# Seven block products for the global projection, and a new layout of SBUF, in a planned one-core transformer kernel

## The chip, the cores and the metric

The kernel runs as one program on one core of a Trainium2 chip. The metric is the device time of one execution in microseconds (us), from the first to the last instruction and the little that lies around them; the median of three runs stands for the kernel. Everything is fp32.

## What is computed

Eight sequences `x[b]` of 512 tokens by 256 channels pass through a feed-forward stack of two layers, then a global attention, then the same stack once more:

```python
x = x + 0.5 * ffn(layernorm(x))        # two layers, called "first" below
x = x + attn(layernorm(x), weight)     # 16 heads of 16 channels, all 512 x 512 scores
x = x + 0.5 * ffn(layernorm(x))        # the same weights again, "second"

# one layer of ffn
qkv = shift_token(x) @ wqkv            # 256 -> 3 x 512, 8 heads of 64
q, k = rotary(l2norm(q) * qs), rotary(l2norm(k) * ksc)
x = x + local_attention(q, k, v) @ wo  # window of 128 and the 128 before it
x = x + (a * gelu(g)) @ w2 + b2        # a, g = split(layernorm(shift_token(x)) @ w1 + b1), 682 wide

# attn: y = layernorm(x), head h
o_h = softmax(y_h @ y_h.T / 4) @ y     # 512 x 256
out = sum over h of o_h @ weight[256 h : 256 h + 256]
```

`shift_token` moves half of the channels by one token. The kernel uses that `o_h @ weight_h` is `softmax @ (y @ weight_h)`: for each of 8 x 16 = 128 heads it projects y (512 x 256) with a 256 x 256 block of `weight` first, and multiplies by the probabilities afterwards.

## The kernel before, in words

**Three flows of work.** `stream(0)` and `stream(1)` (line 950) each take the blocks (0, first), (2, first), (4, first), (0, second), (6, first), (2, second), (4, second), (6, second), plus the stream's number: stream 0 has the even sequences, stream 1 the odd. A block is a layer norm and two layers; a layer is `attention` (line 588) and `glu` (line 833). `global_heads(b)` (line 971) runs for b = 0 to 7, once sequence b has had its first block; a second block waits until its sequence has been through the global part. So in the first and in the last blocks only the two streams are there, and between them the global heads fill the engines.

**One order, written by a planner.** Everything is first recorded as operations, not issued. `Plan.order` (line 272) then simulates the five engines with fixed prices (`cost`, line 235: for instance a signal between engines at 250 ns, a DMA at 170 bytes a ns of shared pipe) and issues the operations in that order. On the chip each engine runs its own list strictly in order and waits on semaphores. Operations recorded under `plan.together()` are one piece. Rank (the place in the recording, plus `plan.shift`) decides between operations that are ready together. All instructions are issued at line 385, so every row of the profile says L385; tiles are told apart by name. Tiles live in rings (`Ring`, line 94): `bufs` slots under one tag, handed out when the last user of a slot is planned to be done.

**DMAs** all go through the queue of SyncE (SP), in the planned order.

**The global projection.** For head h, `front` (line 990) loads the 256 x 256 weight block (`work_wa`), `scores` makes four 128 x 512 score banks and exponentiates them on ScalarE into `work_e`, and `project(half)` (line 1013), called twice, writes 128 x (2 x 256) products y @ weight_h into one PSUM bank that VectorE copies to `work_xw`. `attend` (line 1032) multiplies the probabilities by `work_xw`, 16 matmuls a head, and VectorE adds the result to x in SBUF. An fp32 matmul is two passes of TensorE, each with its own weight load; a transpose is one pass. So one head has 16 passes for the projection with 256 columns each, 32 of 256 columns in `attend`, and 8 of 512 columns on 16 rows, four side by side, for the scores.

**Near and far.** `far` (line 959) picks, for all but the first and last blocks of a stream, a way of transposing that leaves TensorE out: VectorE transposes blocks of 32 x 32 and DMAs through DRAM (`dram_turned`, `dram_quarters`, `dram_later`) put the blocks in place. In the first and the last block (near), `attention` and `glu` transpose on TensorE against `const_ident`. A near `glu` has 16 transposes: 4 that bring the shifted half to token columns, 4 back (`work z` into `sh`), 8 for the normed input.

**What SBUF holds.** x of six sequences (`LIVE = 6`) stays in SBUF from load to output; both layers' `wqkv`, `wo` and rotary tables stay for the whole run; `w1`, `w2` are loaded anew for each of the 16 steps. The probabilities (`work_p0`, `work_p1`) and the q, k tiles (`work_qn0`, `work_qn1`) have two buffers per stream.

**The start.** Loads go out as x0, the q part of wqkv, the rotary table, the scales of q and k, the vectors, the k and v parts, wo, x1, the weights of glu. The scales lie in buffers of the z ring. GpSimd (POOL) multiplies the table by the scales, four instructions per layer (lines 1089 to 1091); only then does the z buffer with the scales come free for the shifted half of the layer's input, whose first column GpSimd sets to zero (`shifted`, line 531).

Of the kernel before, what the change touches and what calls it, by code (L numbers as in the profile page):

```python
# [31 lines left out]
LAG = 6  # L32
SMALL = 4
LIVE = 6
# [142 lines left out]
class Plan:  # L177
# [94 lines left out]
    def order(self):  # L272
# [50 lines left out]
        while len(order) < len(self.ops):  # L323
            best = None
            for e in self.ENGINES:
                when = []
                hold = min((op.rank for op in candidates[e] if len(op.opens) > 4 and op.ready <= free[e]), default=None)
                for op in candidates[e]:
                    if op.opens:
                        at = slots(op)  # L330
                        if at is None:
                            continue
                        if hold is not None and op.rank > hold and op.opens[0].ring.space == PSUM:
                            continue
                        at = max(at, op.ready, free[e])
                    else:
                        at = max(op.ready, free[e])
                    when.append((at, op))
                if when:
                    t = min(at for at, _ in when)  # L340
                    if best is None or t < best[0]:
                        best = t, e, when
            assert best is not None, "the plan is stuck"
            t, e, when = best
            change = self.MODE.get(mode[e], 0.0) if e == "tensor" else self.TABLE if e == "scalar" else 0.0
            switch = lambda op: change if op.mode is not None and op.mode != mode[e] else 0.0
            near = [c for c in when if c[0] <= t + 40]
            if e == "tensor":
                near = gathered(near, when, t)
            at, op = min(near, key=lambda c: (c[1].rank + (self.STICK[e] if switch(c[1]) else 0), c[0]))  # L350
            candidates[e].remove(op)
            op.start = at + switch(op)
            mode[e] = op.mode or mode[e]
            free[e] = op.start + op.busy
            op.end = op.start + op.done
            if op.calls[0][0] == "dma_start":
                a = op.calls[0][2]["out"]
                pipe = max(pipe, op.start + 2000.0) + elements(a) * a.shape[0] * 4 / 170
                op.end = pipe + 300
            for x in op.opens:  # L360
                _, x.slot = x.ring.free.pop(0)
                x.ring.open(x.stream, x.turn)
            for x in op.tiles:
                x.left -= 1
                x.end = max(x.end, op.end)
                if not x.left:
                    x.ring.free.append((x.end + self.SIGNAL, x.slot))
                    x.ring.free.sort()
            for o in op.before:
                if o.engine != e:  # L370
                    o.ready = max(o.ready, op.end + self.SIGNAL)
                elif e != "tensor":
                    o.ready = max(o.ready, op.end)
            for o in op.before + op.admits:
                o.waits -= 1
                if not o.waits:
                    candidates[o.engine].append(o)
            order.append(op)
# [13 lines left out]
def macaron(ctx: ExitStack, tc: tile.TileContext, x, weight, wqkv, wo, w1, w2, b2, vecs, qk_scales, rotary, out):  # L392
# [10 lines left out]
    xs = {}  # L403

    def load_x(b):
        xs[b] = xpool.tile([P, NT, D], F32, tag="x", name=f"x{b}", bufs=LIVE)
        nc.sync.dma_start(out=xs[b], in_=x[b].rearrange("(t p) c -> p t c", p=P))

    def load_attention(l):

        wq = wpool.tile([P, 2, 3 * INNER], F32, tag=f"wqkv{l}", name=f"wqkv{l}")
        for part in range(3):
            if part == 1:
                load_tables(l)
            cols = slice(part * INNER, (part + 1) * INNER)
            nc.sync.dma_start(out=wq[:, :, cols], in_=wqkv[l, :, cols].rearrange("(k p) f -> p k f", p=P))
        o = wpool.tile([P, NPAIR, D], F32, tag=f"wo{l}", name=f"wo{l}")
        nc.sync.dma_start(out=o, in_=wo[l].rearrange("(k p) f -> p k f", p=P))
        return wq, o
# [21 lines left out]
    tabs = [const.tile([P, NT, 2, 2, DH], F32, tag=f"tab{l}", name=f"tab{l}") for l in range(DEPTH)]  # L441
    scales, vec = [], []

    def load_tables(l):

        if l == 0:
            nc.sync.dma_start(out=tabs[-1].rearrange("p t a s d -> p (t a s d)"), in_=rotary)
        sc = zpool.tile([P, 2, 2, DH], F32, tag=f"z{l}", bufs=2, width=N + 1)
        nc.sync.dma_start(out=sc.rearrange("p a s d -> p (a s d)"), in_=qk_scales[l : l + 1, :].partition_broadcast(P))
        scales.append(sc)  # L450
        ve = const.tile([P, NVEC], F32, tag=f"vec{l}", name=f"vec{l}")
        nc.sync.dma_start(out=ve, in_=vecs[l])
        vec.append(ve)

    load_x(0)
    attention_weights = [load_attention(0)]
    load_x(1)
    glu_weights = [load_glu(0)]
    attention_weights.append(load_attention(1))

# [127 lines left out]
    def attention(k, y, l, far):  # L588
        wqkv_sb, wo_sb = attention_weights[l]
# [4 lines left out]
        v, latest = {}, []  # L594
# [3 lines left out]
        def front(t):  # L598
# [4 lines left out]
            tb = tabs[l][:, t]  # L603
            pair = {}
            for part in (1, 0, 2):
                ps = bank([P, INNER])
                with plan.together():
                    for c, z in ((0, z0), (1, z1)):
                        nc.tensor.matmul(
                            ps, lhsT=z[:, tok], rhs=wqkv_sb[:, c, part * INNER : (part + 1) * INNER], start=(c == 0), stop=(c == 1)  # L610
# [8 lines left out]
                qk = work.tile([P, HEADS, 2, half], F32, tag=f"qn{k}", bufs=2)  # L619
# [32 lines left out]
        def scores(t, pair, rn):  # L652
# [21 lines left out]
            for g in range(2):  # L674
# [25 lines left out]
                if far and t > 0:  # L700
                    plan.ops[-1].after.update(latest)
                heads = slice(4 * g, 4 * g + 4)

                if far:
                    nb = 6 if quarters else 4
                    pg = work.tile([P, 2 * N], F32, tag=f"p{k}", bufs=2, width=2 * N)
# [3 lines left out]
                else:  # L710
                    pg = work.tile([P, 4, nk * P], F32, tag=f"p{k}", bufs=2, width=2 * N)
# [44 lines left out]
        def values(t, probs):  # L756
# [25 lines left out]
            if far:  # L782
                for g in range(2):
                    with plan.together():
# [5 lines left out]
                    latest[g:] = [plan.ops[-1]]  # L790
# [42 lines left out]
    def glu(k, y, step, xb, far):  # L833
# [3 lines left out]
        if far:  # L837
            sh = work.tile([P, NT, P], F32, tag=f"qn{k}", bufs=2)
# [12 lines left out]
        if far:  # L851
            hn = work.tile([P, 2, 4, NT, P // 4], F32, tag=f"p{k}", bufs=2, width=2 * N)
            part = lambda c, t: hn[:, c, :, t, :]
            split = lambda u: u.rearrange("p (b c) -> p b c", c=P // 4)
        else:
            hn = work.tile([P, 2, NT, P], F32, tag=f"p{k}", bufs=2, width=2 * N)
# [22 lines left out]
        for m in range(FULL):  # L879
            if m < 4:  # L880
                if m % 2 == 0:
                    pair = work.tile([P, 2, N], F32, tag=f"p{k}", bufs=2)
                u = pair[:, m % 2]
            else:
                u = work.tile([P, N], F32, tag=f"qn{k}", bufs=2)
# [14 lines left out]
        u = work.tile([P, N], F32, tag=f"qn{k}", bufs=2)  # L900
# [49 lines left out]
    def stream(k, blocks):  # L950

        for n, (b, second) in enumerate(blocks):
            while second and (b, True) not in done:
                next(others, None)
            y = layernorm(xs[b], k)
            yield
            for l in range(DEPTH):
                step = DEPTH * n + l
                far = FAR and 0 < n < len(blocks) - 1
                yield from attention(k, y, l, far)  # L960
                yield from glu(k, y, step, xs[b], far)
# [3 lines left out]
                if l == 0 and n + 1 < len(blocks) and blocks[n + 1][0] not in xs:  # L965
                    load_x(blocks[n + 1][0])
            done.add((b, False))
            if second:
                nc.sync.dma_start(out=out[b].rearrange("(t p) c -> p t c", p=P), in_=xs[b])

    def global_heads(b):
        mv, rstd = layernorm_stats([[xs[b][:, t, :]] for t in range(NT)], gsmall)
        ys = []
        for t in range(NT):
            y = work.tile([P, D], F32, tag="e", bufs=2 * NT, width=N)
            normalize(y, xs[b][:, t, :], mv, rstd, t)
# [10 lines left out]

        def front(h):  # L990

            w = work.tile([P, 2, D], F32, tag="wa", bufs=2)
            nc.sync.dma_start(out=w, in_=weight[h * D : (h + 1) * D, :].rearrange("(c p) f -> p c f", p=P))

# [18 lines left out]
            def project(half):  # L1013
                pv = bank([P, 2, D])
                with plan.together():
                    for i in range(2):
                        s = 2 * half + i
                        for c in range(2):
                            nc.tensor.matmul(
                                pv[:, i, :],  # L1020
                                lhsT=zT[c][:, s * P : (s + 1) * P],
                                rhs=w[:, c, :],
                                start=(c == 0),
                                stop=(c == 1),
                            )
                xv = work.tile([P, 2, D], F32, tag="xw", bufs=4)
                nc.vector.tensor_copy(xv, pv)
                xw.append(xv)

            return es, xw, rsum, (scores, lambda: project(0), lambda: project(1))  # L1030

        def attend(head, t):
# [7 lines left out]
            xt = xs[b][:, t, :]  # L1040
# [5 lines left out]
        for h in range(AH + 1):  # L1046
            for t in range(NT):
                if head is not None:
                    attend(head, t)
                if after is not None and t < 3:  # L1050
# [8 lines left out]
            after = front(h + 1) if h + 1 < AH else None  # L1059

# [28 lines left out]
    for l in range(DEPTH):  # L1089
        for t in range(NT):  # L1090
            nc.gpsimd.tensor_mul(tabs[l][:, t], tabs[-1][:, t], scales[l])
# [77 lines left out]
```

## Time and profile before

| what | value |
|---|---|
| median of 3 runs (lowest, highest) | 3890.17 us (3888.96, 3890.24) |
| the profiled execution: its own time | 3893.43 us |
| its span, first to last instruction | 3891.7 us |
| granted TensorE clock, mean over the span | 0.997 |
| TensorE passes, weight loads | 26240, 26240 |
| projection `work_wa, work_gz`: 2048 passes of 256 columns | 476.4 us busy |
| `attend`: 4096 passes of 256 columns | 932.3 us busy |
| transposes on TensorE: 1152 passes of 128 columns | rows `const_ident` |
| DMA traffic | 400.22 MB, mean 103 GB/s |

The busy time of a group of matmuls is the union of its records, and a matmul's record goes on until its result has left the array (382 ns for 256 columns), while the next pass has long begun. So what a pass costs TensorE is read from the distance between starts, in the timeline, and not from the record's length. Times in a timeline are us from the start of the span.

### The profile page before, as it was taken

The page shows a single profiled execution, that of the slowest core. Times are in us where ns is not written, and L with a number is a line of the kernel's source. Part 1 is how long each engine was busy: PE and PEld are TensorE (multiplying, and loading weights), DVE is VectorE, ACT ScalarE, POOL GpSimd, SP SyncE. Part 2 cuts the span into 40 slices and gives each one's busy share as a digit, 9 for nine tenths or more (in the row PEclk, how much of TensorE's full clock was granted, in tenths as well). Part 3 has the DMA queues.
Part 4 walks back from the last instruction along what each step waited for, and adds up shares of the span by engine and source line. Part 5 has one row for each costly group of instructions (what it writes and reads, how often), then busy time and mean ns, then how long its engine had stood idle before and what let it go on. Part 6 is the DMA issues. An engine that isn't in the chain of part 4 may idle for free.

```text
span 3891.7 us, 72922 instructions
## 1 busy us (share of the span) xinstructions
PE 3833.0 (98%) x26240; PEld 2652.3 (68%) x26240; DVE 2460.8 (63%) x6888; ACT 1776.2 (46%) x4559; POOL 1256.3 (32%) x1132
## 2 busy tenths in 40 slices
PE   8999999999999999999999999999999999999998
PEld 4666776776766767767667677676776776767665
DVE  8676755757547467476485665755747657556673
ACT  6665443525435335354254452443533535434663
POOL 6242423415225124142151431522514324223240
PEclk9999999999999999999999999999999999999999
DMA  3001452524524425345254252442543524510000
GB/s 113 1 24 36 144 143 93 158 88 136 143 79 140 125 83 157 94 141 149 70 159 132 91 160 76 135 140 82 156 121 109 157 88 144 146 56 7 1 24 12
DMA packets 437501, 400.22 MB, mean 103 GB/s; under 512 B 53938, under 2 KB 379156, under 8 KB 437140
## 3 DMA queue, kind: packets, MB, share of 16 engines
q1 hardware_dynamic: 437140, 395.56, 33.9%
q8 instruction: 208, 3.41, 0.4%
q14 instruction: 153, 1.25, 0.1%
HBM read 234.96 MB, written 143.66 MB: 97 GB/s over the span
## 4 chain that ended last, share of the span: by engine, by line
PE 61%; DVE 3%; ACT 2%; issue 2%; DMA 1%; SPq 1%; POOL 0%; POOLq 0%; DVEq 0%; ACTq 0%
PE psum_bank L385 61%; ACT work_p L385 2%; DVE work_p L385 1%; SPq L385 1%; DVE work_qn L385 1%; DVE small_ss L385 0%; DVE work_both L385 0%; ACT work_qn L385 0%; DVE ypool_y L385 0%; DMA work_p<-dram_turned 0%; DVE work_o L385 0%; POOL small_rn L385 0%; DMA work_both<-dram_turned 0%; ACT work_sq L385 0%; ACT work_both L385 0%
## 5 line engine op out<-in xcount | busy, mean ns | idle before, releaser
L385 PE MATMUL psum_bank<-work_xw,work_e 128*128 128x256 f32 x4096 | 932.3, 382 | 1.4 <-DVE xpool_x L385 0.8
L385 PEld LDWEIGHTS psum_bank<-work_xw,work_e 128*128 128x128 f32 x4096 | 766.7, 190 | 186.4 <-issue 39.0
L385 PE MATMUL psum_bank<-wpool_wqkv,zpool_z 128*128 128x512 f32 x1536 | 706.5, 600 | 2.0 <-DMA wpool_wqkv<-in_wqkv_dram 1.3
L385 ACT ACTIVATE work_p<-work_p,small_nmax,small_rn 128x192 f32<-128x192 f32 (+2 forms) x1024 | 543.0, 532 | 184.6 <-DVE small_nmax L385 136.8
L385 POOL TENSOR_TENSOR work_t<-work_qn,const_tab 128x256 f32<-128x256 f32 x512 | 419.8, 841 | 587.7 <-ACT work_qn L385 554.8
L385 PE MATMUL psum_bank<-zpool_z,wpool_w 128*128 128x512 f32 x1280 | 559.3, 595 | 0.6 <-DVE zpool_z L385 0.6
L385 POOL TENSOR_TENSOR small_rn<-small_ss,const_nhalf 128x8 f32<-128x8 f32 x256 | 489.2, 1913 | 148.0 <-DVE small_ss L385 130.8
L385 POOL TENSOR_TENSOR work_p<-work_p,small_ri 128x768 f32<-128x768 f32 (+1 forms) x192 | 264.0, 1377 | 807.9 <-DVE small_ri L385 433.6
L385 PEld LDWEIGHTS psum_bank<-wpool_wqkv,zpool_z 128*128 128x128 f32 x1536 | 282.9, 191 | 291.7 <-issue 268.3
L385 PE MATMUL psum_bank<-work_wa,work_gz 128*128 128x256 f32 x2048 | 476.4, 381 | 0.0
L385 ACT ACTIVATE work_e<-psum_bank 128x512 f32<-128x512 f32 x512 | 298.3, 595 | 345.2 <-PE psum_bank L385 344.7
L385 PEld LDWEIGHTS psum_bank<-zpool_z,wpool_w 128*128 128x128 f32 x1280 | 243.2, 191 | 302.7 <-issue 278.8
L385 PEld LDWEIGHTS psum_bank<-work_wa,work_gz 128*128 128x128 f32 x2048 | 385.7, 190 | 72.0 <-issue 10.6
L385 DVE SCALAR_TENSOR_TENSOR xpool_x<-psum_bank,gsmall_rinv,xpool_x 128x256 f32<-128x256 f32 x512 | 240.0, 473 | 278.9 <-PE psum_bank L385 277.3
L385 ACT COPY work_o<-psum_bank 128x512 f32<-128x512 f32 x128 | 74.5, 582 | 498.5 <-PE psum_bank L385 490.7
L385 ACT COPY work_qn<-psum_bank 128x512 f32<-128x512 f32 x256 | 147.7, 582 | 334.2 <-PE psum_bank L385 290.0
L385 DVE SCALAR_TENSOR_TENSOR work_p<-psum_bank,const_vec,work_p 128x512 f32<-128x512 f32 x128 | 95.6, 748 | 262.0 <-PE psum_bank L385 201.3
L385 PE MATMUL psum_bank<-wpool_wo,work_o 128*128 128x256 f32 x1024 | 245.2, 383 | 5.8 <-DVE work_o L385 5.6
L385 DVE TENSOR_REDUCE small_ss<-work_sq 128x8 f32<-128x512 f32 x256 | 173.2, 677 | 117.2 <-ACT work_sq L385 116.6
L385 PE MATMUL psum_bank<-wpool_w,work_p 128*128 128x256 f32 x1024 | 243.3, 380 | 0.0
L385 DVE COPY work_xw<-psum_bank 128x512 f32<-128x512 f32 x256 | 173.0, 680 | 105.9 <-PE psum_bank L385 104.5
L385 PEld LDWEIGHTS psum_bank<-wpool_wo,work_o 128*128 128x128 f32 x1024 | 192.5, 190 | 58.1 <-DVE work_o L385 13.7
(90 smaller groups left out, 4951.7 us busy)
## 6 DMA issues: line engine op xcount, KB each, us to landing
work_p<-dram_quarters SPq DMA_DIRECT2D x576, 128.0 KB
dram_quarters<-work_p SPq DMA_DIRECT2D x288, 192.0 KB
dram_turned<-work_both SPq DMA_DIRECT2D x96, 512.0 KB
work_both<-dram_turned SPq DMA_DIRECT2D x384, 128.0 KB
work_wa<-in_weight_dram SPq DMA_DIRECT2D x128, 256.0 KB
wpool_w<-in_w_dram SPq DMA_DIRECT2D x48, 640.0 KB
work_hT<-work_gz SPq DMA_DIRECT2D x512, 32.0 KB
dram_turned<-work_p SPq DMA_DIRECT2D x48, 256.0 KB
```

Of the source, the lines that this page charges most:

```text
L385: getattr(getattr(nc, op.engine), name)(*map(real, args), **{k: real(a) for k, a in kw.items()})
```

## The change

The diff has some 450 lines. Its parts:

1. **Seven block products.** `project(half)` twice becomes one chain of three pieces per head. y (512 x 256) and the weight block (256 x 256) are cut into 2 x 2 blocks; four sums of y blocks are made once per sequence on VectorE (`sums`), four sums of weight blocks per head on GpSimd (`mixed`, and one in place in `work_wa`), and seven products of 256 x 128 by 128 x 128 replace eight. The running sum u is kept in a PSUM bank, read by ScalarE, and added to again by TensorE, three times over. Ranks inside get a shift of -20.

```diff
-            def project(half):
-                pv = bank([P, 2, D])
...
-                xv = work.tile([P, 2, D], F32, tag="xw", bufs=4)
-                nc.vector.tensor_copy(xv, pv)
+            t1, t2, t4 = (mixed[:, i] for i in range(3))
+            nc.gpsimd.tensor_sub(t1, b12, b11)
+            nc.gpsimd.tensor_sub(b12, b22, b12)
+            nc.gpsimd.tensor_sub(t2, b22, t1)
+            nc.gpsimd.tensor_sub(t4, b21, t2)
+            t3 = b12
...
+            def product(to, a, b, start=(True, True)):
+                for i in range(2):
+                    nc.tensor.matmul(
+                        to[:, i, :], lhsT=a[:, i * P : (i + 1) * P], rhs=b, start=start[i], stop=True, skip_group_check=not start[i]
+                    )
...
+                with plan.together():
+                    product(v, a12, b21)
+                    product(u, a11, b11, (True, False))
+                    product(r, s1, t1, (True, False))
+                plan.shift = -20
+                x11 = xw[0][:, :, :P]
+                nc.scalar.copy(x11, u)
+                nc.vector.tensor_add(x11, v, x11)
+                with plan.together():
+                    product(u, s2, t2, (False, False))
...
+                nc.scalar.copy(x12, u)
+                with plan.together():
+                    product(u, s3, t3, (False, False))
+                nc.scalar.copy(x22, u)
+                nc.vector.tensor_add(x22, r, x22)
...
+                with plan.together():
+                    product(u, a22, t4, (False, False))
+                    product(r, s4, b22, (False, False))
+                nc.scalar.copy(x21, u)
+                nc.vector.tensor_add(x12, r, x12)
```

2. **SBUF laid out anew.** x has four buffers (`LIVE = 4`): a stream loads it at the start of a block, once more for the last `glu`, and stores it to DRAM at the end (`keep_x`); the global part loads and stores it likewise. The three parts of wqkv, wo and the rotary table have one set of buffers and are loaded at each of the 16 steps; the two scaled tables are kept in DRAM.

```diff
-LIVE = 6
+LIVE = 4
...
+    def keep_x(b, t):
+        if held[b] is None:
+            held[b] = dram.tile([P, NT, D], F32, tag=f"x{b}", name=f"x{b}")
+        nc.sync.dma_start(out=held[b], in_=t)
...
+            attention_weights.append((load_qkv(l), load_wo(l), tab))
...
-                qk = work.tile([P, HEADS, 2, half], F32, tag=f"qn{k}", bufs=2)
+                qk = work.tile([P, HEADS, 2, half], F32, tag=f"qn{k}", bufs=4)
...
-                    pg = work.tile([P, 2 * N], F32, tag=f"p{k}", bufs=2, width=2 * N)
+                    pg = work.tile([P, 2 * N], F32, tag=f"p{k}", bufs=4, width=2 * N)
```

3. **`glu` is far in all blocks**; `attention` stays near in the first and the last.

```diff
-                yield from glu(k, y, step, xs[b], far)
+                yield from glu(k, y, step, xb, FAR)
```

4. **Far values in one piece.** The products of both groups of four heads are recorded together, and an extra dependency of the scores on the last values (`latest`) is gone.

```diff
-                if far and t > 0:
-                    plan.ops[-1].after.update(latest)
...
-                for g in range(2):
-                    with plan.together():
+                with plan.together():
+                    for g in range(2):
```

5. **The start.** Loads go out as x0, the k, q and v parts, the rotary table, both layers' scales and vectors, wo, x1; GpSimd scales both layers' tables in a row.

```diff
+    def scale_tables():
+        first = new_table()
+        for l in range(DEPTH):
+            t_ = work.tile([P, NT, 2, 2, DH], F32, tag="p1", bufs=4, width=2 * N) if l else first
+            for t in range(NT):
+                nc.gpsimd.tensor_mul(t_[:, t], raw_table[:, t], scales[l])
```

6. **The planner's price of a DMA** goes from 170 to 210 bytes a ns.

## Prediction

> **What bounds the kernel now.** I read the page's busy times and slices first, then the list of what TensorE (PE) waits for, by stage, then the timeline.
>
> ```profile
> PE 3833.0 (98%) x26240; PEld 2652.3 (68%) x26240; DVE 2460.8 (63%) x6888; ACT 1776.2 (46%) x4559; POOL 1256.3 (32%) x1132
> ...
> PE   8999999999999999999999999999999999999998
> ```
>
> PE is busy in every slice; no other engine passes 63%. A busy PE could still be a PE that waits inside records, so I asked for its waits between 300 and 3480 us, where the global heads run beside the two streams:
>
> ```profile
> PE psum_bank L385 <- ACT work_kT L385: 2.3, 4, 0.8
> PE psum_bank L385 <- DVE xpool_x L385: 1.9, 3, 0.8
> PE psum_bank L385 <- ACT work_e L385: 0.8, 2, 0.7
> PE psum_bank L385 <- DVE ypool_y L385: 0.8, 2, 0.4
> PE psum_bank L385 <- DVE work_o L385: 0.7, 3, 0.3
> PE psum_bank L385 <- ACT work_both L385: 0.3, 1, 0.3
> PE psum_bank L385 <- DVE small_peak L385: 0.3, 1, 0.3
> ```
>
> The columns are total us, times, longest. 7 us of waits in 3180: the planned order keeps PE fed, so there a us of PE work is a us of time. The same view gives 27 us for 0 to 300 and 17 us for 3480 to 3892, where only the two streams run. So PE is priced by its passes in the middle, and the ends by their chains.
>
> **1. The projection.** Price of a pass, from two timeline rows (start, length, x passes); a row's length is the distances between starts plus one record:
>
> ```profile
> 1517.19 1.89 PE L385 MATMUL psum_bank<-work_wa,work_gz 128*128 128x256 f32 x8
> ```
> ```profile
> 3704.59 1.04 PE L385 MATMUL psum_bank<-const_ident,work_qn 128*128 128x128 f32 x8
> ```
>
> 256 columns: (1.89 - 0.381)/7 = 0.216 us. 128 columns: (1.04 - 0.277)/7 = 0.109 us, with new 128 x 128 weights for every pass, as the new products need them. Before: 2048 x 0.216 = 442 us. After: 128 heads x 7 products x 2 matmuls x 2 passes = 3584 x 0.109 = 391 us. **-51 us.** It rests on a transpose pass standing for a product pass; both are one weight load and 128 columns.
>
> The Trainium skill speaks against it: "TensorE: Matmul & The Clock Gate", section "Back-to-back issue gap", gives 81 ns sustained for pairs of weight load and matmul at 128 columns and 131 ns at 512, so a column costs 2.5 times as much in narrow passes. Estimated from that page, with 98 ns at 256, the new passes would take 3584 x 0.216 x 81/98 = 640 us, and the kernel would lose some 200 us. Here 512 columns take 0.429 us (a row of 20 passes, 8.75 us long) and 128 take 0.109, one quarter, so I go by the rows.
>
> What surrounds it costs little by occupancy: ACT gains 512 copies at 0.375 (row work_both, 128x256), 192 us on 1776; DVE swaps 256 copies at 0.680 for 384 additions at about 0.417 (row ypool_y), -14 us; POOL gains 512 differences, 0.29 (affine_select 128x128) to 0.42 (half of a work_t row), some 180 us on 1256. All stay under 65%, beside PE work.
>
> **2. New waits of PE.** u is read by ACT and added to again, three times a head, and behind the waiting product stands everything of PE's list. The need, from the trace: 0.17 until the product has left PE, 0.04 to ACT, copy 0.375, 0.05 back, 0.63 us. Where VectorE's addition comes in between too, 0.03 + 0.42 more, 1.09 us. In the changed kernel's built order the PE work put between (priced as above) is mostly 1.09 us (one score group) or 1.73 (an attend); 14 places have under 0.7. But in 65 of the 128 heads the second product waits for the addition that reads v in the same bank, not only for the copy of u: there 1.09 of cover has no slack, and an addition that stands behind one DVE instruction (0.7) is late. The third group always waits for an addition, with 1.47 to 1.73 of cover. Bounds: 0, as the 7 us above suggest for planned waits, to 65 x 0.7 = 45 us. I take **+8**, nearer to the planned-waits row.
>
> **3. Far glu at the ends.** Eight near glus lose 16 transposes each: 128 x 0.109 = **-14 us** of PE. Their chain grows. From the addition to y to the first w1 pass, the near one takes 8.7 us (3845.06 to 3853.73), the far one about 24.6 in a row of the middle (538.12 to about 562.7: two DMA round trips, one 1.23 transpose). With the 3.1 before it (o, wo) it needs 27.7 from the last values. In the built order PE has 20.6, 20.6, 22.0 and 24.3 us of work there for stream 0, and 29.4 to 30.4 for stream 1. Stream 1 is covered; stream 0 is short by 23 in all four, less what the other stream's attention waits anyway, and less the quicker DMAs of a quiet stage (DMA share 0.04 against 0.40). Bounds 0 to 23, I take **+6**.
>
> The last glu before stood bare:
>
> ```profile
> 3845.54 0.47 PE L385 MATMUL psum_bank<-const_ident,ypool_y 128*128 128x128 f32 x1 [0.52 <-DVE ypool_y L385]
> 3846.89 0.63 PE L385 MATMUL psum_bank<-const_ident,zpool_z 128*128 128x128 f32 x4 [0.88 <-DVE zpool_z L385]
> 3850.63 2.52 PE L385 MATMUL psum_bank<-const_ident,work_p 128*128 128x128 f32 x8 [3.10 <-DVE work_p L385]
> 3853.73 16.44 PE L385 MATMUL psum_bank<-zpool_z,wpool_w 128*128 128x512 f32 x31 [0.58 <-DVE zpool_z L385]
> ```
>
> Brackets: idle before, 5.1 us; and 31 passes take 16.44 instead of 13.5, for the clock is granted at 0.5 for 10.2 us from 3849.3. Now stream 0's whole w1 and w2 (27.7 us) lie over this chain: **-8 us**.
>
> **4. The start.**
>
> ```profile
> 9.45 2.76 POOL L385 TENSOR_TENSOR const_tab<-const_tab,zpool_z 128x256 f32<-128x256 f32 x4 [1.71 <-DMA zpool_z<-in_qk_scales_dram]
> 12.27 0.10 POOL L385 MEMSET zpool_z<- 128x1 f32 x1
> ```
>
> PE's second product (12.49) needs that memset. In the new order the scales lie behind two more loads of 512 KB (2.6 us at the 380 to 410 GB/s of these first us, 4.2 at the pace of k's landing, 2.05 us for 512 KB), and eight multiplications instead of four stand before the memset: 2.76 more. +5.4 to +7.0; +2.8 if the loads hide. I take **+6**. k's own wait (1.30) is inside it.
>
> **5. The rest.** Reloaded wqkv parts have 48 us of PE work between the last use and the next, wo 26, against some 5 us for 512 KB: nothing, covered by the other stream's work. x goes out and in at a block's ends: some 10 us more before a second block; the least PE work between the last attend and the layer norm's transposes that need it is 17 us, so nothing; without that cover it would be 10. Traffic rises from 395 to 471 MB on SP's queue and its issues from 2623 to 2808, at a DMA share of 34%. Of POOL's queue: the four differences stand ahead of rotary and pow rows, which have planned room. The 210 in the planner makes a landing 0.6 us earlier in the plan than before: in 2's and 3's bounds. Tile-shape changes of PE fall from 692 to 670, at 0.10 each (1505.71 to 1507.53 holds four passes of 0.429), **-2**. Four buffers of p, q and k and the dropped dependency can only take from the 27 and 17 us at the ends: 0 to -10, counted at 0.
>
> **Sum** on the profiled execution: -51 + 8 - 14 + 6 - 8 + 6 - 2 = -55; 3893.4 - 55 = 3838.4. That execution lies 3.3 above the median, so **3835 us**.
>
> **Rivals.**
> *A, the ends take it back* (still faster): the far chains and the start at their upper bounds and the last glu's gap only moved to stream 0: +17 + 1 + 8 on the forecast, 3861. For: the covers of 20.6. Against: both ends have attention waits that the longer chain hides.
> *B, PE stands at u* (slower): 384 products wait in order for ACT or DVE. ACT does runs of eight exponentials (0.53 each, 1516.03 to 1520.3); a copy behind half of one is 2 us late. The 63 us gained elsewhere are lost at 63/384 = 0.16 us a wait; at a mean of 0.35, +134 - 8, 3961. For: 65 heads without slack. Against: 7 us of planned waits now.
> *C, narrow passes are bound by weight loads* (slower): a load's record is 190 ns. At 0.190 a pass 681 us, +290 on the forecast, 4125; it decides from 0.109 + 55/3584 = 0.124. Against: the row of eight at 0.109.
> *D, the gain isn't there*, because the plan had slack elsewhere: 3890. Against: 98% in the middle.
>
> **Chances.** Forecast 0.74, A 0.15, B 0.06, C 0.02, D 0.03. Within 0.2% (7.8 us, about what a measurement can tell): D, 0.03; slower: B, C, 0.08; faster 0.89. Range: all terms at their good ends and -10 for the buffers, 3808; at the other side A with 11 us more of part 2, 3872.
>
> **What would show it.** The projection's passes 0.109 apart; 7 to 20 us of PE waits in the middle, on ACT or DVE work_xw; the second product near 18.5 us; a gap before stream 0's last w1 and none before stream 1's. Wrong it would be if work_xw heads PE's waits with over 60 us, or passes lie over 0.12 apart.

## The result, and the profile after

The changed kernel takes 3897.22 us (median of 20 runs, 3893.72 to 3901.64) against 3891.01 us (20 runs, 3888.96 to 3895.01) for the kernel before: a ratio of 1.0016, 95% interval 1.0010 to 1.0022. The forecast was 3835, its range 3808 to 3872. TensorE's passes became cheaper much as forecast, and the time did not follow. Where a run has its own time below, it is the median; spans and rows are of one profiled execution each.

The page of the changed kernel, busy times and TensorE's slices:

```profile
PE 3798.8 (98%) x27648; PEld 2684.7 (69%) x27648; DVE 2463.9 (63%) x7048; ACT 1910.5 (49%) x5053; POOL 1494.0 (38%) x1636
...
PE   8999999999999999999999999999999999999998
```

PE's busy time fell by 34 us and its share stayed at 98%. ACT rose by 134 us and POOL by 238. Taken against the old projection (the first experiment below), so for the products alone, ACT has 142 us more where the prediction had 192, POOL 238 where it had 180, and VectorE (DVE), which was to lose 14, has 5 more. What PE waits for between 300 and 3480 us (total us, times, longest):

```profile
PE psum_bank L386 <- DVE work_xw L386: 13.9, 23, 1.9
PE psum_bank L386 <- DVE work_o L386: 7.4, 8, 1.6
PE psum_bank L386 <- ACT work_xw L386: 6.7, 7, 2.2
PE psum_bank L386 <- DVE zpool_z L386: 2.6, 3, 1.3
PE psum_bank L386 <- ACT work_kT L386: 1.1, 2, 0.6
```

All lines of this view add up to 35 us, against 7 before. The products' own line, work_xw, has 20.6 of them. One head's products in the timeline (start, length, passes):

```profile
1500.75 1.05 PE L386 MATMUL psum_bank<-work_wa,work_gz 128*128 128x128 f32 x8
1501.64 0.61 PE L386 MATMUL psum_bank<-work_mixed,work_sums 128*128 128x128 f32 x4
1502.09 1.89 PE L386 MATMUL psum_bank<-work_xw,work_e 128*128 128x256 f32 x8
```

Four passes start 1502.09 - 1501.64 = 0.45 us before what follows, 0.112 a pass; over all such groups the median distance is 0.112, and 0.109 for the transposes that stood in for them. The start, on POOL and then PE:

```profile
11.83 2.76 POOL L386 TENSOR_TENSOR const_tab<-work_p,zpool_z 128x256 f32<-128x256 f32 x4 [3.95 <-DMA zpool_z<-in_qk_scales_dram]
14.55 2.77 POOL L386 TENSOR_TENSOR work_p<-work_p,zpool_z 128x256 f32<-128x256 f32 x4
17.25 0.14 POOL L386 MEMSET zpool_z<- 128x1 f32 x2
```
```profile
17.41 9.44 PE L386 MATMUL psum_bank<-wpool_wqkv,zpool_z 128*128 128x512 f32 x18 [4.52 <-POOL zpool_z L386]
```

The scales land 2.4 us later and eight multiplications stand before the memset: the second product comes at 17.41 instead of 12.49. The last w1 of stream 1:

```profile
3856.06 17.33 PE L386 MATMUL psum_bank<-zpool_z,wpool_w 128*128 128x512 f32 x40
```

No gap before it, and 40 passes in 17.33 us, 0.43 each: the bare gap and the slowed clock of before are gone. Stream 0's last w1 has a gap, as was named: 1.29 us, at 3828.43.

**An account of PE's time.** I added up the distances between the starts of successive passes: passes on the whole array at their usual distance (0.216 for 256 columns, 0.432 for 512, 0.112 or 0.109 for 128), changes of tile shape and groups of small tiles at theirs, and what is beyond as stalls. (The median distance at 512 columns is 0.429; the 2816 such passes are in all three kernels, so the differences between the columns of the table do not hang on it.) "Old projection" is the first experiment below. In us:

| | before | old projection | changed |
|---|---|---|---|
| passes on the whole array | 3227.3 | 3213.3 | 3171.0 |
| changes of tile shape | 149.8 | 136.0 | 143.1 |
| groups of small tiles | 415.9 | 423.0 | 428.6 |
| stalls | 83.9 | 102.5 | 134.6 |
| of these between 370 and 3550 us | 21.9 | 34.8 | 69.5 |
| first attend to last attend | 3182.1 | 3177.7 | 3181.7 |

56 us of passes went, 51 us of stalls came, 48 of them in the middle. The wait view shows some 28 of the 48: it counts idle time only behind the modelled end of the last record, and it does not see passes that run on a slower clock. Such passes are there:

```profile
1234.96 1.14 PE L386 MATMUL psum_bank<-work_hT 16*128 16x512 f32 x8
...
1238.29 0.68 PE L386 MATMUL psum_bank<-work_mixed,work_gz 128*128 128x128 f32 x4 [2.19 <-ACT work_xw L386]
...
1239.68 2.09 PE L386 MATMUL psum_bank<-work_hT 16*128 16x512 f32 x8
```

Eight passes for the scores take 1.14 us before the wait and 2.09 behind it: from 1238.9 the clock is granted at 0.5 for 6.8 us. In the middle of this execution it is at 0.5 for 20.4 us in four pieces, which takes some 10 us of PE's time, most of it among the 48; in the kernel before it is at 1.0 all through the middle. Three of the four pieces begin within 1 us behind the three longest waits there, 2.19, 1.94 and 1.82 us, all on work_xw. So a long wait cost more than its own length, and neither the prediction nor the wait view has that part. Over the twenty executions of the changed kernel the mean clock goes from 0.997 to 0.993, and those two took 3893.72 and 3901.64 us.

The last row of the table, "the middle" below, is the distance from the first pass of `attend` to the last.

### The profile page after: what moved, and what is told of

The parts are those of the page before. It is cut to its first block, busy times and chain, and to the rows that moved or that the text cites. A ratio compares the mean times of both kernels' runs of the same rounds, so it can differ in the third digit from the quotient of the medians.

```text
span 3892.1 us, 76868 instructions
## 1 busy us (share of the span) xinstructions
PE 3798.8 (98%) x27648; PEld 2684.7 (69%) x27648; DVE 2463.9 (63%) x7048; ACT 1910.5 (49%) x5053; POOL 1494.0 (38%) x1636
## 4 chain that ended last, share of the span: by engine, by line
PE 51%; DVE 6%; ACT 3%; issue 2%; POOL 1%; DMA 1%; SPq 0%; DVEq 0%; ACTq 0%; POOLq 0%
PE psum_bank L386 51%; ACT work_p L386 2%; DVE work_p L386 2%; DVE work_qn L386 1%; DVE small_ss L386 1%; POOL small_rn L386 0%; SPq L386 0%; POOL work_t L386 0%; DVE work_both L386 0%; DMA dram_quarters<-work_p 0%; DVE xpool_x L386 0%; ACT work_both L386 0%; DVE work_xw L386 0%; DMA work_hT<-work_gz 0%; ACT work_qn L386 0%
## 5 line engine op out<-in xcount | busy, mean ns | idle before, releaser
L386 PE MATMUL psum_bank<-work_xw,work_e 128*128 128x256 f32 x4096 | 952.5, 382 | 2.6 <-DVE work_xw L386 1.6
L386 ACT COPY work_xw<-psum_bank 128x256 f32<-128x256 f32 x512 | 188.5, 371 | 574.5 <-PE psum_bank L386 547.5
L386 DVE TENSOR_TENSOR work_xw<-psum_bank,work_xw 128x256 f32<-128x256 f32 x384 | 159.7, 417 | 163.3 <-PE psum_bank L386 59.0
L386 POOL TENSOR_TENSOR work_mixed<-work_wa 128x128 f32<-128x128 f32 x128 | 63.5, 496 | 457.1 <-DMA work_wa<-in_weight_dram 422.6
L386 DVE STREAM_TRANSPOSE work_p<-work_p 128x768 f32<-128x768 f32 (+2 forms) x224 | 211.4, 946 | 15.6 <-POOL work_p L386 14.7
```

What stands on the lines that cost most here:

```text
L386: getattr(getattr(nc, op.engine), name)(*map(real, args), **{k: real(a) for k, a in kw.items()})
```

## Experiments

**Theories at the start.** *Theory 1*: the accumulating products make PE stand in order behind reads of u, v and r, and narrow passes are dearer. *Theory 2*: the products are worth their forecast, and the layout, the start and the reordered plan took it back.

**Old projection.** Undoes part 1 alone.

```diff
-            def product(to, a, b, start=(True, True)):
...
+            def project(half):
+                pv = bank([P, 2, D])
```

> The changed kernel with the old projection (eight products, two copies by VectorE a head), and everything else of the change kept: layout, far glu, far values in one piece, start, planner price. Theory 1 (the products give some 50 us less PE work and lose nearly all of it in waits of PE at the accumulating products and in passes of 0.112 instead of 0.109): undoing them costs little, 3885 to 3910 us. Theory 2 (the products are worth the forecast -43, and the layout, the start and the reordered plan took it back): 3930 to 3945 us.

3890.11 us, ratio to before 0.9996 (0.9987 to 1.0005). Theory 2 falls, as far as one order can show it: in this order parts 2 to 6 together are worth nothing, and the products cost 7 us.

**v beside r.** In the built order of the changed kernel, 65 heads' second products wait for VectorE's read of v in u's bank.

```diff
-                one, two = bank([P, 2, 2, P]), bank([P, 2, P])
-                regions.extend((one[:, 0], one[:, 1], two))
+                one, two = bank([P, 2, P]), bank([P, 2, 2, P])
+                regions.extend((one, two[:, 0], two[:, 1]))
```

> The changed kernel with v, the product that VectorE alone reads, put into the bank of r instead of the bank of u. The order of the instructions on every engine stays the same, only bank numbers change. So the second product into u waits for ScalarE's copy of u alone. Theory 1: the 13 us of stalls at that product and some of the 9 us behind it go, 3875 to 3888 us. Theory 2: within 5 us of 3897.

3887.43 us, ratio 0.9989 (0.9980 to 0.9998): 10 us below the changed kernel, at the weak end of what was expected. The wait view, 300 to 3480 us:

```profile
PE psum_bank L386 <- DVE work_o L386: 11.0, 10, 2.2
PE psum_bank L386 <- ACT work_xw L386: 6.7, 8, 2.2
PE psum_bank L386 <- DVE work_xw L386: 3.6, 5, 1.0
```

VectorE's work_xw lost 10.3 us, work_o took 3.6 up. The Trainium skill, "PSUM — Partial Sum Buffer", section "Terms", says that two engines may not be on the same bank and the same quadrant of partitions at once, which is a reason for a product into u to wait for a read of v beside it; the fall from 23 waits to 5 agrees.

**Slack of 500.**

```diff
             op.busy, op.done = self.cost(op)
+            if any(t.ring.name == "xw" for t in op.tiles) and op.engine in ("scalar", "vector") and len(op.after) and op.calls[0][0] in ("copy", "tensor_add"):
+                op.done += 500
```

> The changed kernel, with one line added in the planner: what ScalarE and VectorE read out of the product banks into work_xw is priced to end 500 ns later, so that more PE work is put between a product and the next one into the same region. Theory 1: most of the 41 us of stalls at the products go, 3855 to 3880 us. Theory 2: within 5 us of the changed kernel's 3897.

3918.03 us, ratio 1.0066 (1.0053 to 1.0078). Against both theories: room that the planner leaves at the products has to be filled with other work, and the new order is worse.

**No reads between.**

```diff
-                x11 = xw[0][:, :, :P]
-                nc.scalar.copy(x11, u)
-                nc.vector.tensor_add(x11, v, x11)
                 with plan.together():
                     product(u, s2, t2, (False, False))
...
                     product(r, s4, b22, (False, False))
+                nc.scalar.copy(x11, u)
+                nc.vector.tensor_add(x11, v, x11)
+                nc.scalar.copy(x12, u)
+                nc.scalar.copy(x22, u)
```

> The changed kernel with all seven products of a head recorded before the first read: the three copies that ScalarE made between products into u, and the additions, come after the last product. So u is read as one full sum four times, which is another sum than the projection; the number and shape of the instructions is the same on every engine. No product waits for a read of u, v or r any more. Theory 1 (waits of PE at u): the 40 us of stalls at the products go, 3850 to 3870 us. Theory 2 (the products' time is lost elsewhere, for instance to queues that run later because ScalarE and GpSimd have more to do): above 3880 us.

3890.0 us, ratio 0.9995 (0.9986 to 1.0004). By the account above, the stalls at the products went, those before `attend` (work_xw, work_e) rose from 15 to 28 us, and others came elsewhere; seven reads now stand between the last product and the first `attend`. Theory 1 loses its size, but the order is a new one.

**Same order, no waits.** So the order was kept, and the operands changed when the instructions are issued: `other` puts a tile of SBUF in the place of u, v or r.

```diff
                 nc.scalar.copy(x11, u)
+                other(u)
                 nc.vector.tensor_add(x11, v, x11)
+                other(v)
```

> The changed kernel in its own planned order, instruction for instruction on every engine, but the reads between the products (two copies and the copy before the third group by ScalarE, two additions by VectorE, per head) take their PSUM operand from a finished tile in SBUF instead of u, v and r; so those parts of the projection are not computed. No product waits for a read any more, and the plan is not made anew. Theory 1 (waits of PE at u in order): 3850 to 3862 us, about 3897 minus the 35 to 40 us of stalls at the products. If these stalls only stand in for waits that would come later on the same list: above 3880 us.

3892.98 us, ratio 1.0004 (0.9995 to 1.0013), 4 us below the changed kernel, which is about the width of the intervals. The work is not quite the same: with the operand in SBUF 384 of the copies take 406 ns on average instead of 371, and 256 of the additions 527 instead of 417; the page has VectorE 21 us busier than in the changed kernel, ScalarE about as busy. By the price that the short reads give below (22 us for 184 us of work) that hides some 3 us, an estimate; the waits would then be worth some 7 us, not 35 to 40. Theory 1 loses its size here too: most of the waits stood in for others. Where PE now waits (300 to 3480 us):

```profile
PE psum_bank L389 <- DVE work_o L389: 13.2, 13, 2.5
PE psum_bank L389 <- DVE xpool_x L389: 5.1, 7, 1.2
```

And one of those waits, 2.20 us on PE up to 1119.17, seen on VectorE:

```profile
1114.92 0.47 DVE L389 SCALAR_TENSOR_TENSOR xpool_x<-psum_bank,gsmall_rinv,xpool_x 128x256 f32<-128x256 f32 x1
1115.32 0.82 DVE L389 TENSOR_TENSOR work_qn<-work_qn,work_t 128x512 f32<-128x512 f32 x1
1116.06 0.67 DVE L389 TENSOR_REDUCE small_ss<-work_sq 128x8 f32<-128x512 f32 x1
1116.66 0.41 DVE L389 TENSOR_TENSOR work_xw<-work_gz,work_xw 128x256 f32<-128x256 f32 x1
...
1118.10 0.68 DVE L389 TENSOR_TENSOR work_qn<-work_qn,small_rn 128x512 f32<-128x512 f32 x1
1118.70 0.41 DVE L389 TENSOR_TENSOR work_o<-psum_bank,work_o 128x256 f32<-128x256 f32 x1
```

Each row starts before the one ahead has ended, the left-out ones included, and none has an idle time in brackets: VectorE, 63% busy over the span, is full for 4 us, and the addition that PE needs has its place in the list. *Theory 3*: the work that the products put on VectorE and ScalarE, in lists that are full in stretches, eats the gain; GpSimd's is off the path.

**Parts undone singly**, on the kernel with v beside r: the far values in two pieces, the old order of the start, near glu at the ends.

```diff
-                with plan.together():
-                    for g in range(2):
+                for g in range(2):
+                    with plan.together():
```
```diff
-    first_qkv = load_qkv(0)
-    raw_table = load_tables()
+    first_qkv = load_qkv(0, load_tables)
...
+    scale_table(1)
```
```diff
-                yield from glu(k, y, step, xb, FAR)
+                yield from glu(k, y, step, xb, far)
```

> The kernel with v beside r, and part 4 undone: the far values in two pieces and the scores held back behind the last values. In the trace with v beside r, waits for the additions to work_o are 18 us in the middle, against 3 us in the kernel before. If the one piece makes those waits, 3875 to 3880 us against the 3887 of v beside r; if the waits belong to the denser plan of the products, no change (within 4 us).

3929.26 us, 42 above v beside r, all of it in the middle (3169.1 to 3211.5).

> The kernel with v beside r, and part 5 undone in its order: behind x0 and the k part come the rotary table and the scales of layer 0 alone, GpSimd multiplies four times before the memset, and the table of layer 1 is scaled six stages later. If the start costs the 6 us that the prediction gave it, 3881 us; if the streams wait for something later anyway, no change.

3898.03 us, 11 above. The second product came at 13.17, the memset's wait was gone, and the stretch from PE's first pass to the first attend grew from 373.7 to 386.2, as it would if the streams wait for something later; the other four multiplications now stand at 34.9 us in GpSimd's list, between rotary work.

> The kernel with v beside r, and part 3 undone: glu near in the first and the last blocks. The prediction put far glu there at -16 us (-14 transposes, +6 chain, -8 last gap): then this is 3903 us. If the far chains at the first blocks take as much as the last blocks gain, it is 3887, no change.

3916.1 us, 29 above: 3.1 in the start, 12.9 in the end, and 17.6 in the middle, which has the same work. So each single step back costs 11 to 42 us, while all of parts 2 to 6 together, the kernel before against the old projection, are worth nothing. With a new order each, these runs measure orders as much as parts.

**Other orders of the same work.** How large are the accidents of an order?

```diff
-    SIGNAL = 250.0
+    SIGNAL = 246.0
```

> The changed kernel, with the planner's price of a signal at 246 ns instead of 250: the same work, another order. It tests how much of the result hangs on the one order that the planner happened to find. If the order's accidents are small, within 4 us of 3897; if they are of the size of the forecast gain, off by 10 to 30 us, either way.

> The changed kernel, with the planner's price of a signal at 254 ns. As with 246: within 4 us of 3897 if the order's accidents are small, off by 10 to 30 us if not.

> The kernel before, with the planner's price of a signal at 246 ns. If the orders of the kernel before have accidents of the same size, 10 us or more from 3891; if its order is only harder to disturb, within 5 us.

3900.94 us and 3893.58 us for the changed kernel (+4 and -4), 3899.68 us for the one before (+8). Less than the lost 62, and about as much as the difference between the two kernels: a difference of 6 us says nothing about their parts.

**Is a us of PE a us?** From here the planned orders stay as they are and single instructions are made shorter when they are issued.

```diff
+                plan.ops[-1].instead = [
+                    (name, (args[0][:, :224], *args[1:]), {**kw, "rhs": kw["rhs"][:, :224]}) for name, args, kw in plan.ops[-1].calls
+                ]
```

> The kernel before, in its own order, with each projection matmul cut from 256 to 224 columns; the last 32 columns are not computed. VectorE's copies, every wait and every other instruction stay (the eight PSUM banks are zeroed once at the start). That takes 2048 x 0.027 = 55 us from TensorE and nothing from any other engine, as much as the products were to take. If a us of TensorE is a us of time in the middle, as the prediction read it: 3836 us. If VectorE and ScalarE bound parts of the middle already: 3845 to 3870 us.

3845.37 us, ratio 0.9881 (0.9866 to 0.9896): 46 us for 55, 0.84 of a us each, and the middle 46.3 shorter. The reading of the profile before was nearly right: an edit that takes 55 us from PE and gives nothing to the others would have come some 10 us from the forecast.

**Short reads, short differences.**

```diff
                 nc.scalar.copy(x11, u)
+                plan.ops[-1].instead = x11[:, :, :8], u[:, :, :8]
```
```diff
             nc.gpsimd.tensor_sub(t1, b12, b11)
+            plan.ops[-1].instead = t1[:, :8], b12[:, :8], b11[:, :8]
```

> The changed kernel in its own order, with the seven reads of the products per head (four copies by ScalarE, three additions by VectorE) cut to 8 of 128 columns; the rest of the projection is not written (its tiles are zeroed once at the start). Every wait stays, only the reads are short. Theory 3 (the work of these reads on VectorE and ScalarE, in queues that are full in stretches, is what eats the gain): 15 to 25 us less than the changed kernel, 3872 to 3882. If only waits count, as little as taking the waits away did (-4): 3890 or more.

3875.03 us, ratio 0.9957 (0.9942 to 0.9973): 22 us below the changed kernel with every wait in place, where taking the waits away gave 4. Only four executions stand behind it, two at 3870 us and two at 3880 and 3881, so 22 is good to some 6 us. The page has VectorE 85 us and ScalarE 99 us less busy; the middle is 25.4 us shorter. Short reads also end earlier: the waits at work_xw fall from 20.6 to 12.9 us, and the time at half clock in the middle from 20.4 to 6.8 us. So the 22 us are the price of the reads in all, their place in the lists and what PE waits for them together, and the run does not part the two.

> The changed kernel in its own order, with GpSimd's four differences of weight blocks per head cut to 8 of 128 columns, so the mixed blocks are not computed beyond them (their tiles are zeroed once at the start). It takes some 180 us from GpSimd. If GpSimd's new work slows VectorE or delays the products, 10 us or more below 3897; theory 3 has GpSimd off the path: within 5 us.

3886.83 us, ratio 0.9987 (0.9978 to 0.9996): 10 us below, twice the 5 us at most that theory 3 gave GpSimd: it is not off the path. The page has GpSimd 131 us less busy (a difference cut to 8 columns still takes 0.236). What of VectorE changes with it is seen in these rows, first of the changed kernel, then of this run (count, busy us, mean ns):

```profile
L386 DVE TENSOR_TENSOR work_qn<-work_qn,const_tab 128x512 f32<-128x512 f32 x256 | 188.6, 737 | 6.3 <-POOL work_t L386 5.7
L386 DVE TENSOR_REDUCE small_ss<-work_sq 128x8 f32<-128x512 f32 x256 | 172.9, 676 | 96.2 <-ACT work_sq L386 95.7
```
```profile
L396 DVE TENSOR_TENSOR work_qn<-work_qn,const_tab 128x512 f32<-128x512 f32 x256 | 185.1, 723 | 3.3 <-POOL work_t L396 2.6
L396 DVE TENSOR_REDUCE small_ss<-work_sq 128x8 f32<-128x512 f32 x256 | 173.0, 676 | 96.9 <-ACT work_sq L396 96.4
```

The multiplication, with two inputs in SBUF, takes 704 ns with the old projection, 737 with the differences, 723 with short ones; the reduction, with one, 676 each time. The Trainium skill, "SBUF — State Buffer", section "SBUF: two separate sides", says that VectorE's second port is also GpSimd's, and that an instruction with two SBUF inputs and one of GpSimd that reads SBUF shut each other out for their whole length. The rows agree in direction; 33 ns x 256 = 8 us of VectorE is what they show here, not how much of it reaches the end.

**Light side engines, in both kernels.** Seven kinds of VectorE's operations and the global exponentials do a quarter of their columns.

```diff
+                plan.ops[-1].instead = qf[:, :few], qf[:, :few], tb[:, 0, part].unsqueeze(1).to_broadcast([P, few, DH])
...
+                    plan.ops[-1].instead = e[:, :P], sps[s][:, :P], AF.Exp
```

> The changed kernel in its own order, all of TensorE's and DMA's work as it is, with lighter side engines: the rotary multiplications and additions of q and k, the additions to x, y and o on VectorE, and the exponentials of the global scores on ScalarE do a quarter of their columns. Theory 3 (VectorE and ScalarE bound stretches of the middle): 30 to 50 us less, 3847 to 3867. If TensorE alone bounds: no change, 3897 less 0 to 5.

> The kernel before with the same lighter side engines. Theory 3: it gains too, 25 to 40 us, 3851 to 3866, for the side engines already bound stretches of it; the reading of 7 us of waits says no more than 7 us.

3839.98 us (ratio to before 0.9866, 0.9852 to 0.9881) and 3853.83 us (0.9904, 0.9887 to 0.9921). The changed kernel gains 57, more than expected, the one before 38. The sizes fit the theory, but the place does not for the kernel before: its middle is only 11.9 us shorter, start and end 28.5, whereas the changed kernel's middle is 34.0 shorter. So in the middle the side engines bound little before, and 22 us more after. With light side engines the changed kernel is 14 us the faster of the two.

**A version below both.** If lists that run late are the cause, an order with less lateness has to pay.

```diff
-    SIGNAL = 250.0
+    SIGNAL = 247.0
...
-    PATIENCE, LINGER = 10000.0, 250.0
+    PATIENCE, LINGER = 10000.0, 300.0
...
-                plan.shift = -20
+                plan.shift = -40
```

> The kernel with v beside r, and three constants of the planner moved: signal 247, patience with a tile shape 300, shift -40. They were picked among some 350 settings by replaying each order with the durations of the traces (ScalarE's short exponentials 0.1 us longer than the planner's price, passes of 0.112). If VectorE's and ScalarE's queues decide, an order in which they are less late is worth 8 to 13 us: 3874 to 3880, below both kernels.

> The kernel with v beside r, and only the planner's price of a signal moved, 250 to 241. By the same replay 9 us less than 3887: 3876 to 3882.

3874.57 us, ratio 0.9959 (0.9945 to 0.9973), 16 us below the kernel before and 23 below the changed one; and 3886.53 us, ratio 0.9989 (0.9981 to 0.9998), no gain over v beside r where 5 to 11 us were expected. One hit of two: the replay ranks orders roughly, within some 10 us. The hit was picked among some 350 orders, so it agrees with theory 3 but does not show it.

## Why the prediction was wrong, step by step

**The failed step** is the end of part 1: "All stay under 65%, beside PE work", which costed the products' work on the other engines at nothing. Cutting that work to a stub gives 22 us back (reads, with what PE waits for them) and 10 us (differences, only half of which could be cut), in the order of the changed kernel: some 32 of the 62 us that are missing. The sizes were off as well: a difference takes 0.492 us, where 0.29 to 0.42 was read. Busy shares over the span can't show the cost: all did stay under 65%, as the prediction says. The place of an instruction in a full list shows it.

**Part 1, -51.** Right in kind, 10 us too large: 3584 x 0.112 = 401, so -41. Rival C's 0.124 was not reached, and the Trainium skill's ratio of 2.5 per column ("TensorE: Matmul & The Clock Gate", section "Back-to-back issue gap"), which the prediction set against the rows, does not hold for these fp32 passes: 0.112 us for 128 columns stands against 0.216 for 256 and 0.429 for 512.

**Part 2, +8.** The waits at work_xw are 20.6 us in the wait view, about the 7 to 20 that were named. Taken away in the same order they give 4 us, with reads that take longer, and moving v to the bank of r alone gives 10, so +8 was about the right size. The half clock behind the three longest, some 8 us, was in no bound. Rival B's mechanism is there, at 20.6/384 = 0.054 us a product (0.11 by the 41 us of stalls that the expectations count) where it was priced at 0.35, and it is not the main cause. The sign set for being wrong, over 60 us at work_xw, never came, though the forecast fell: it looked for the loss under one name, while the stalls had many.

**Part 3, -16.** Start and end of the run with near glu are 3.1 and 12.9 us longer: 16. The sum of the step was right; its three terms were not measured apart. The 17.6 us in the middle, where the work is the same, are put down to another order.

**Part 4, +6.** The second product came 4.9 us later; with the old order it came early again and the time rose by 11 us, so the second product's time is not what the start hangs on.

**Part 5.** The dropped dependency (with the buffers 0 to -10, counted at 0) and the far values in one piece, which the prediction gives no price, are worth 42 us in the order with v beside r; how much of that is the order is not known, and with the other parts they sum to nothing.

**Rival D** has the time nearly right and the reason wrong: the plan before had little slack, as 0.84 of each us of PE came through.

**The sum for the products.** From the old projection to the changed kernel 42.3 us of passes go (table), at 0.84 -36; reads with their waits +22, differences at least +10: about -4, measured +7. The rest of 11 is little more than an order's accident; the table has 13 us more for shapes and small tiles there. Effects taken away one at a time need not add up, so the split is an estimate from these runs.

**Open.** Why parts 2 to 6, forecast at -12, sum to -1, since each run that undid one made another order. The profiles say where: from PE's first pass to the first attend it takes 360.0 us before and 372.8 with the old projection, from the last attend to PE's last pass 334.7 and 324.4. The end gave about what was forecast, and the start took it back; neither the old order of the start (386.2) nor near glu (376.8, against 373.7) makes that stretch shorter. Open too are the products in the layout of the kernel before: there is no time for them, since their pool of tiles needs 109 KB a partition there and 107.47 are left.

## What to carry to other kernels

When work moves off the bound engine, price what it puts on the others by their lists and not by their busy share: find the stretches where those lists run without a gap, and ask what stands behind the new instructions there. Test with the order kept, by making one engine's instructions shorter; here taking the waits away mostly moved them. In a kernel whose order a planner writes, run two or three orders of the same work first: a difference below their spread (here up to 8 us) is no verdict on an edit. And look at the granted clock behind long waits of TensorE, since a wait view does not show what the clock takes.

## What the runs showed of the hardware that was not expected

- Product passes of 128 columns are 0.112 us apart, transposes 0.109.
- In the changed kernel the three longest waits of TensorE in the middle, 1.82 to 2.19 us, were each followed within 1 us by 3.4 or 6.8 us at half clock.
- VectorE's additions of 128 x 256 take 0.417 us with one operand in PSUM and 0.527 on average with both in SBUF (same order, no waits).
- ScalarE's exponentials with a bias, a scale and a sum follow each other at 0.477, 0.531 and 0.585 us for 128, 192 and 256 columns (distances of back-to-back starts in the changed kernel): the line through them meets 0 columns at 0.37 us, an estimate. Those of 512 columns, which read PSUM and have no bias, take 0.570, less than the 256 with one.
- A GpSimd difference of 128 x 128 takes 0.492 us on average and 0.236 with 8 columns: cutting 120 of 128 columns saves about half.
